# Folding the opening weights in another order, and splitting the late weights' preparation over two steps, in a two-layer fp32 pair kernel

## Chip, cores and metric

The kernel runs on one core of a Trainium2 chip. The metric is the device time of one execution in microseconds (us). Before the change four runs gave a median of 3333.75 us (3333.4 to 3334.44). Besides them there is one profiled execution, from which every duration below is taken.

The engines are named as the profile names them: PE is the matmul engine (TensorE) and PEld its weight loads, DVE is VectorE, ACT is ScalarE, POOL is GpSimd, SP is SyncE. A name with a "q" behind it (ACTq, SPq) is the engine's instruction queue, where DMA issues are shown.

## What is computed

`x` is a 384 x 384 field of 128 channels in fp32. Two layers follow each other:

```python
# layer 0
z = layernorm(x, norm_g, norm_b)
left  = (z @ Wl + bl) * sigmoid(z @ Wlg + blg)
right = (z @ Wr + br) * sigmoid(z @ Wrg + brg)
core  = einsum('bikh,bjkh->bijh', left, right)
zo    = layernorm(core, onorm_g, onorm_b) @ Wout + bout
x     = x + sigmoid(x @ Wg + bg) * zo
# layer 1
left  = x @ W_left + b_left + (x @ W_eq + b_eq)
right_sum = sum over the row of (x @ W_right + b_right)
out   = left * right_sum * sigmoid(x @ W_gate + b_gate)
out   = out @ W_out + b_out
y     = layernorm(out + x, ln_scale, ln_bias)
```

## The kernel before, in words

The work falls into three stages. Stage 1 (about 15 to 1146 us) makes `left` and `right` of layer 0; stage 2 (to 1889 us) is the einsum, channel by channel (L385 to L406); stage 3 is the rest, row by row (L610 to L663). The order of each engine's instructions is written out by hand: `seq` (L56) keeps program order on every engine.

Stage 1 reads `x` in 144 chunks of 8 tiles of 128 x 128 (`load_chunk`, L109) and works in 288 steps of 4 tiles, two steps to a chunk. For a step (n, q):

- `stats` (L215): mean and variance of the 4 tiles on DVE, in two halves.
- `powers` (L227): on POOL, the reciprocal root `rs` of the variance, by a power of -1/2, and `nd`, the mean less the root itself. It runs once for a chunk, at its second step, on 8 tiles.
- `shift` (L241): on POOL, z = x - nd, from two z buffers.
- `front` (L251): PE transposes z into a PSUM tile `pt` (two buffers), and ACT copies it to `zt`.
- `back` (L282), in two halves: PE multiplies `zt` with `wz`, the four weights side by side (L291), into a tile `pr` (three buffers); ACT takes the sigmoid of the gate half (L298); DVE multiplies both halves and the root into `lr` (L300).

The main loop (L328) runs, for step k: `shift` of step k+2, `powers` of k+5, `back` of k in two halves, with `front` of k+1 between them and `stats` of k+6 after each half. Then come SP's transfers: a chunk's load, the store of `zt`, a slice of `lr`. Ahead of the loop, six steps' statistics are taken (L316 to L327).

Two pieces of preparation lie around this:

- **The opening.** The layer norm's scale and shift are folded into the weights. ACT's queue issues the loads of the four weights, two columns (norm_g, norm_b), the four biases (one row each) and the chunks 2 to 5 (L129 to L135); only after that ACT loads its function table and warms it up (L144). `fold` (L148) on DVE brings weights and biases from the order l, r, lg, rg into pairs (l and r interleaved, then the gates), and PE adds up p1, the weights' column part with m1 = avg x (norm_b - norm_g), and the biases. `weights` (L164) makes wz = weights x norm_g + p1. All of the staging lies in one SBUF tile `stage`. `fold` comes after the second step's statistics, `weights` after the third's.
- **The late weights.** The weights of the later stages are loaded at step 4 (L346). After step 20, `late_weights` (L190) prepares them: on DVE m2 = -avg x onorm_g, on PE its product with Wout, on DVE wc from that, on PE Wout x onorm_b, on DVE bz; W_left += W_eq, and for each of three biases a product on PE and a subtraction on DVE. All five products go into one PSUM tile `pw`, which takes a `pt` buffer; m2 takes a z buffer.

Of the kernel before, what the change touches and what calls it, by code (L numbers as in the profile page):

```python
# [8 lines left out]
F32 = mybir.dt.float32  # L9
# [10 lines left out]
def triangle_then_gated_row_kernel(ctx: ExitStack, tc: tile.TileContext, a: dict, out: bass.AP):  # L20
# [35 lines left out]
    def seq(ins):  # L56

        return tc.keep_in_program_order(ins)
# [4 lines left out]
    def load(dst, src, queue=nc.sync):  # L63
        seq(queue.dma_start(out=dst, in_=src))
# [15 lines left out]
    with ExitStack() as ctx2:  # L80
# [15 lines left out]
        with tc.tile_pool(name="p1x", bufs=6, side="right") as xp, \  # L96
# [25 lines left out]


            stage = lrp.tile([P, H, G, 2], F32, tag="lr", name="stage").rearrange("p h i s -> p (h i s)")
            wst, wcat = stage[:, 0:4 * H], stage[:, 4 * H:8 * H]
            bst, bcat = stage[0:1, 8 * H:12 * H], stage[0:1, 12 * H:16 * H]
            m1, d = stage[:, 16 * H:17 * H], stage[:, 17 * H:17 * H + 1]
            sides = ("l", "r", "lg", "rg")
            for n, w in enumerate(sides):  # L129
                load(wst[:, n * H:(n + 1) * H], a["L0_conv_W" + w], nc.scalar)  # L130
            g0, b0 = column("L0_conv_norm_g", nc.scalar), column("L0_conv_norm_b", nc.scalar)
            for n, b in enumerate(sides):
                load(bst[:, n * H:(n + 1) * H], a["L0_conv_b" + b].rearrange("(o h) -> o h", o=1), nc.scalar)
            for n in range(2, 6):
                load_chunk(n, nc.scalar)  # L135
            ident = const([P, P], "ident")
# [6 lines left out]
            warm = const([P, 1], "warm")  # L143
            seq(nc.scalar.activation(warm, mhalf[:, 0:1], AF.Sigmoid))  # L144
            wz = const([P, 4 * H], "wz")
            p1 = pps.tile([P, 2, 4 * H], F32, tag="pr", name="p1")

            def fold():  # L148

                for t, st in ((wcat, wst), (bcat, bst)):  # L150
                    for g in range(2):
                        seq(nc.vector.tensor_copy(
                            t[:, g * 2 * H:(g + 1) * 2 * H].rearrange("p (h s) -> p s h", s=2),
                            st[:, g * 2 * H:(g + 1) * 2 * H].rearrange("p (s h) -> p s h", s=2),
                        ))

                seq(nc.vector.tensor_sub(d, b0, g0))
                seq(nc.vector.tensor_scalar(m1, avg, d, None, ALU.mult))  # L160
                seq(nc.tensor.matmul(p1[:, 0], lhsT=m1, rhs=wcat, start=True, stop=False))
                seq(nc.tensor.matmul(p1[:, 0], lhsT=avg[0:1, :], rhs=bcat, start=False, stop=True))

            def weights():  # L164
                seq(nc.vector.scalar_tensor_tensor(wz, wcat, g0, p1[:, 0], ALU.mult, ALU.add))

            wc = const([P, C], "wc")
            bz = const([P, 1], "bz")
# [21 lines left out]
            def late_weights():  # L190

                ps = tps.tile([P, 4, P], F32, tag="pt", name="pw")
                m2 = wp.tile([P, 4, C], F32, tag="z", name="m2", bufs=2)[:, 0]
                seq(nc.vector.tensor_scalar(m2, avg, go, -1.0, ALU.mult, ALU.mult))
                seq(nc.tensor.matmul(ps[:, 0], lhsT=m2, rhs=wout0, start=True, stop=True))
                seq(nc.vector.scalar_tensor_tensor(wc, wout0, go, ps[:, 0], ALU.mult, ALU.add))
                seq(nc.tensor.matmul(ps[:, 1, 0:1], lhsT=wout0, rhs=bo, start=True, stop=True))
                seq(nc.vector.tensor_add(bz, ps[:, 1, 0:1], bout0))  # L200

                seq(nc.vector.tensor_add(wleft, wleft, weq))
                seq(nc.vector.tensor_add(bleft, bleft, beq))
                for n, (w, b) in enumerate(((wleft, bleft), (wgate, bgate), (wright, bright))):
                    p4 = ps[:, 2, n:n + 1]
                    seq(nc.tensor.matmul(p4, lhsT=w, rhs=bout1, start=True, stop=True))
                    seq(nc.vector.tensor_sub(b, b, p4))
                seq(nc.vector.tensor_scalar(bright, bright, float(N), None, ALU.mult))  # L210

                seq(nc.vector.tensor_scalar(lns, lns, -1.0, None, ALU.mult))


            def stats(n, q, half):  # L215
# [11 lines left out]
            def powers(n, q):  # L227


                if q == NQ - 1:  # L230
                    _, mv, rs, sd = normed[n]
                    kb, ig, c = chunks[n]
                    if c == 0:
                        nds[kb, ig] = dp.tile([P, G], F32, tag="nd", name="nd")
                    nd = nds[kb, ig][:, c * XR:(c + 1) * XR]
                    seq(nc.gpsimd.tensor_scalar(sd, mv[:, :, 1], EPS, 1.0, ALU.add, ALU.mult))  # L236
                    seq(nc.gpsimd.tensor_tensor(rs, sd, mhalf[:, :XR], ALU.pow))
                    seq(nc.gpsimd.tensor_tensor(sd, sd, rs, ALU.mult))
                    seq(nc.gpsimd.tensor_tensor(nd, mv[:, :, 0], sd, ALU.subtract))

            def shift(n, q):  # L241

                kb, ig, c = chunks[n]
                z = wp.tile([P, 4, C], F32, tag="z", name="z", bufs=2)
                nd = nds[kb, ig][:, c * XR + 4 * q:c * XR + 4 * q + 4]
                seq(nc.gpsimd.tensor_tensor(  # L246
                    z, loaded[n][:, 4 * q:4 * q + 4, :], nd.unsqueeze(2).to_broadcast([P, 4, C]), ALU.subtract
                ))
                return z
# [66 lines left out]
            for k in range(AHEAD):  # L316
                for half in range(2):
                    stats(*steps[k], half)
                if k == 1:
                    fold()  # L320
                if k == 2:
                    weights()
                if k < AHEAD - 1:
                    powers(*steps[k])
                if k == 1:
                    zs = {j: shift(*steps[j]) for j in range(2)}
                    front(*steps[0], zs.pop(0))  # L327
            for k, (n, q) in enumerate(steps):  # L328
                if k + 2 < len(steps):
                    zs[k + 2] = shift(*steps[k + 2])  # L330
                if k + AHEAD - 1 < len(steps):
                    powers(*steps[k + AHEAD - 1])
                for half in range(2):
                    back(n, q, half)
                    if half == 0 and k + 1 < len(steps):
                        front(*steps[k + 1], zs.pop(k + 1))
                    if k + AHEAD < len(steps):
                        stats(*steps[k + AHEAD], half)
                if q == NQ - 1:
                    del loaded[n], normed[n]  # L340
                    load_chunk(n + 6)
                    if chunks[n][2] == G // XR - 1:
                        store_nd(*chunks[n][:2])
                store_zt(n, q)
                store_slice()
                if k == 4:  # L346
                    for t, src in later:
                        load(t, src)
                if k == 20:
                    late_weights()  # L350
                if k == len(steps) - 2 * G // 4 + 16:
                    assert not full
                    for h in range(2):
                        load_h(h)
# [338 lines left out]
```

## Time and profile before

| | us |
|---|---|
| median of four runs | 3333.75 (3333.4 to 3334.44) |
| profiled execution, its own time | 3332.9 |
| its span, first to last instruction | 3330.8 |
| PE busy | 3284.5 (99%) |
| DVE, POOL, ACT busy | 2499.2 (75%), 2234.8 (67%), 1949.5 (59%) |
| first matmul of L291 starts | 15.41 |
| late weights: first and last product start | 101.58, 105.49 |

The page of a profile gives busy times by engine, the chain of work that ended last, and the costliest groups of instructions; a row of a group ends in the idle time of the engine just before it and in what ended that idle time ("<-"). A row of the timeline is: start, duration, engine, line, operation, output<-inputs, shape, count ("x4" is four in a row), and in brackets the idle time before it. Matmuls in fp32 are recorded as two instructions each, and they overlap, so their spacing is read from the starts.

### The profile page before, as it was taken

The page shows a single profiled execution, that of the slowest core. Times are in us where ns is not written, and L with a number is a line of the kernel's source. Part 1 is how long each engine was busy: PE and PEld are TensorE (multiplying, and loading weights), DVE is VectorE, ACT ScalarE, POOL GpSimd, SP SyncE. Part 2 cuts the span into 40 slices and gives each one's busy share as a digit, 9 for nine tenths or more (in the row PEclk, how much of TensorE's full clock was granted, in tenths as well). Part 3 has the DMA queues.
Part 4 walks back from the last instruction along what each step waited for, and adds up shares of the span by engine and source line. Part 5 has one row for each costly group of instructions (what it writes and reads, how often), then busy time and mean ns, then how long its engine had stood idle before and what let it go on. Part 6 is the DMA issues. An engine that isn't in the chain of part 4 may idle for free.

```text
span 3330.8 us, 48534 instructions
## 1 busy us (share of the span) xinstructions
PE 3284.5 (99%) x12584; PEld 2005.5 (60%) x12584; DVE 2499.2 (75%) x8074; ACT 1949.5 (59%) x4049; POOL 2234.8 (67%) x3267
## 2 busy tenths in 40 slices
PE   8999999999999999999999999999999999999997
PEld 4444444444444566666666566777777777777775
DVE  6677777777777655554555578888888888888887
ACT  4455555555555433433433567777777777777776
POOL 5455555555555466555555378888888888888887
PEclk9999999999999999999999999999999999999999
DMA  5899899899999498999999888889888988998883
GB/s 150 241 282 283 251 282 278 257 282 272 263 281 266 146 284 284 281 282 285 281 284 285 273 266 249 270 274 276 265 272 274 272 269 272 276 269 269 274 269 95
DMA packets 924619, 872.93 MB, mean 262 GB/s; under 512 B 24868, under 2 KB 839720, under 8 KB 924344
## 3 DMA queue, kind: packets, MB, share of 16 engines
q1 hardware_dynamic: 904960, 794.32, 76.3%
q0 software_dynamic: 13152, 71.37, 10.5%
q10 hardware_dynamic: 6232, 4.13, 0.4%
q8 instruction: 103, 1.69, 0.2%
q14 instruction: 172, 1.41, 0.1%
HBM read 507.85 MB, written 361.89 MB: 261 GB/s over the span
## 4 chain that ended last, share of the span: by engine, by line
PE 62%; ACT 1%; POOL 1%; DVE 0%; issue 0%; DMA 0%; POOLq 0%; SPq 0%; ACTq 0%
PE pc L392 22%; PE pr L530 7%; PE py L559 7%; PE pg L493 7%; PE pl L548 7%; PE pg L547 7%; PE py L560 4%; ACT py L590 1%; POOL rs L579 0%; PE pq L514 0%; DMA xt<-nd_d 0%; POOL yt L602 0%; PE pxt L506 0%; DVE yt L601 0%; DVE st L574 0%
## 5 line engine op out<-in xcount | busy, mean ns | idle before, releaser
L291 PE MATMUL pr<-wz,zt 128*128 128x512 f32 x2304 | 1042.7, 594 | 0.7 <-ACT zt L257 0.7
L298 ACT ACTIVATE sg<-pr,rs 128x256 f32<-128x256 f32 x1152 | 482.7, 470 | 508.1 <-PE pr L291 375.4
L392 PE MATMUL pc<-rr,lrh 128*128 128x384 f32 x2304 | 743.3, 486 | 1.9 <-DVE lr L300 1.9
L300 DVE SCALAR_TENSOR_TENSOR lr<-pr,rs,sg 128x256 f32<-128x256 f32 x1152 | 504.7, 480 | 275.0 <-ACT sg L298 227.1
L291 PEld LDWEIGHTS pr<-wz,zt 128*128 128x128 f32 x2304 | 415.2, 191 | 412.4 <-issue 346.8
L392 PEld LDWEIGHTS pc<-rr,lrh 128*128 128x128 f32 x2304 | 452.0, 196 | 293.2 <-issue 2.5
L590 ACT ACTIVATE py<-py,nm,rs 128x128 f32<-128x128 f32 x1152 | 494.4, 429 | 184.0 <-POOL rs L583 90.4
L401 DVE TENSOR_TENSOR csum<-csum,ct 128x1152 f32<-128x1152 f32 x128 | 178.9, 1398 | 347.1 <-ACT ct L398 347.1
L559 PEld LDWEIGHTS py<-wo,u 128*128 128x128 f32 x2304 | 377.5, 191 | 102.4 <-ACT wo L541 1.7
L398 ACT COPY ct<-pc 128x1152 f32<-128x1152 f32 x128 | 143.2, 1119 | 450.4 <-PE pc L392 446.7
L602 POOL TENSOR_TENSOR yt<-yt,lnb 128x384 f32<-128x384 f32 x384 | 404.8, 1054 | 2.9 <-DVE yt L601 2.6
L521 POOL TENSOR_TENSOR cs<-ct,rt 128x384 f32<-128x384 f32 x384 | 405.0, 1059 | 0.9 <-PE pr L530 0.9
L559 PE MATMUL py<-wo,u 128*128 128x128 f32 x2304 | 403.0, 275 | 1.2 <-ACT wo L541 1.2
L378 POOL COPY rr<-lrh 128x768 f32<-128x768 f32 x128 | 176.2, 1376 | 309.0 <-DMA lrh<-lr_d 299.8
L574 DVE BATCH_NORM_STATS2 st<-py 128x6 f32<-128x128 f32 x1152 | 265.9, 286 | 96.5 <-PE py L560 95.9
L246 POOL TENSOR_TENSOR z<-xt,nd 128x512 f32<-128x512 f32 x288 | 299.8, 1041 | 43.4 <-POOL z L246 30.7
L530 PE MATMUL pr<-cs,wc 128*128 128x384 f32 x768 | 318.8, 497 | 2.9 <-POOL cs L521 2.9
L236 POOL TENSOR_SCALAR sd<-mv 128x8 f32<-128x8 f32 x144 | 28.3, 197 | 436.9 <-DVE mv L225 436.9
L560 PE MATMUL py<-ident,x1T 128*128 128x128 f32 x1152 | 314.0, 273 | 0.0
L548 PE MATMUL pl<-x1T,mat_L_conv_W_left 128*128 128x384 f32 x768 | 311.5, 487 | 1.2 <-ACT gT L495 1.2
L547 PE MATMUL pg<-x1T,mat_L_conv_W_gate 128*128 128x384 f32 x768 | 311.5, 487 | 0.9 <-DVE x1T L533 0.5
L493 PE MATMUL pg<-xt,mat_L_conv_Wg 128*128 128x384 f32 x720 | 292.0, 487 | 0.0
(96 smaller groups left out, 4912.2 us busy)
## 6 DMA issues: line engine op xcount, KB each, us to landing
lr_d<-lr SPq DMA_DIRECT2D x128, 1024.0 KB, 7.2
lrh<-lr_d SPq DMA_DIRECT2D x128, 768.0 KB, 7.8
xt_d<-zt SPq DMA_DIRECT2D x288, 256.0 KB, 5.3
ct<-core_d SPq DMA_DIRECT2D x96, 768.0 KB, 6.6
rt<-rstd_d SPq DMA_DIRECT2D x96, 768.0 KB, 8.1
out_dram<-yt SPq DMA_DIRECT2D x95, 768.0 KB, 4.9
core_d<-ct SPq DMA_DIRECT2D x125, 576.0 KB, 8.8
xt<-in_x_dram SPq DMA_DIRECT2D x140, 512.0 KB, 6.9
```

Of the source, the lines that this page charges most:

```text
L291: seq(nc.tensor.matmul(pr[:, r, :], lhsT=zts[n, q][:, 2 * half + r, :], rhs=wz, start=True, stop=True))
L298: seq(nc.scalar.activation(sg[r], pr[:, r, 2 * H:], AF.Sigmoid, scale=rs[r]))
L300: seq(nc.vector.scalar_tensor_tensor(t[:, :, c * XR + r0 + r, :], pr[:, r, :2 * H].rearrange("k (h s) -> k h s", s=2), rs[r], sg[r].rearra ...
L392: seq(nc.tensor.matmul(pc[:, ib, :N], lhsT=t[:, kb, ib * P:(ib + 1) * P, 0], rhs=rr[:, kb], start=(kb == 0), stop=(kb == NB - 1),))
L493: seq(nc.tensor.matmul(pg[:, :N], lhsT=wg0, rhs=r["xT"], start=True, stop=True))
L521: seq(nc.gpsimd.tensor_tensor(cs, ct[:, i % RG], rt[:, i % RG], ALU.mult))
L530: seq(nc.tensor.matmul(pr[:, :N], lhsT=wc, rhs=r["cs"], start=True, stop=True))
L547: seq(nc.tensor.matmul(pg2[:, :N], lhsT=wgate, rhs=r["x1T"], start=True, stop=True))
L548: seq(nc.tensor.matmul(pl[:, :N], lhsT=wleft, rhs=r["x1T"], start=True, stop=True))
L559: seq(nc.tensor.matmul(py[:, s], lhsT=r["u"][:, s], rhs=r["wo"], start=True, stop=False))
L560: seq(nc.tensor.matmul(py[:, s], lhsT=r["x1T"][:, s], rhs=ident, start=False, stop=True, is_transpose=True))
L590: seq(nc.scalar.activation(py[:, s], py[:, s], AF.Identity, bias=nm[:, n, b:b + 1], scale=rs[:, n, b:b + 1]))
```

## The change

In the opening, the biases are loaded to all 128 partitions, so that each bias load writes 64 KB instead of one row. The weights are no longer re-ordered before the fold: DVE scales the biases by 1/C and computes wst = wst x norm_g + bst in the order loaded, PE makes a single product p1 from m1 and wst, and the pairing happens when `weights` adds the two (two additions). The first chunk's roots are taken for each step by itself, on 4 tiles. `fold` comes after the first step's statistics, `weights` after the second's, and shift and front of step 0 come before the second step's statistics.

The late weights are split. After step 20, DVE makes m2, adds W_eq and b_eq and negates ln_scale. After step 21, PE makes all five products, and DVE then reads them all.

```diff
-            wst, wcat = stage[:, 0:4 * H], stage[:, 4 * H:8 * H]
-            bst, bcat = stage[0:1, 8 * H:12 * H], stage[0:1, 12 * H:16 * H]
-            m1, d = stage[:, 16 * H:17 * H], stage[:, 17 * H:17 * H + 1]
+            wst, bst = stage[:, 0:4 * H], stage[:, 4 * H:8 * H]
+            m1, d = stage[:, 8 * H:9 * H], stage[:, 9 * H:9 * H + 1]
...
-                load(bst[:, n * H:(n + 1) * H], a["L0_conv_b" + b].rearrange("(o h) -> o h", o=1), nc.scalar)
+                load(bst[:, n * H:(n + 1) * H], a["L0_conv_b" + b].partition_broadcast(P), nc.scalar)
...
-            p1 = pps.tile([P, 2, 4 * H], F32, tag="pr", name="p1")
+            p1 = pps.tile([P, 2, 4 * H], F32, tag="pr", name="p1")[:, 0]
 
             def fold():
-
-                for t, st in ((wcat, wst), (bcat, bst)):
-                    for g in range(2):
-                        seq(nc.vector.tensor_copy(
-                            t[:, g * 2 * H:(g + 1) * 2 * H].rearrange("p (h s) -> p s h", s=2),
-                            st[:, g * 2 * H:(g + 1) * 2 * H].rearrange("p (s h) -> p s h", s=2),
-                        ))
                 seq(nc.vector.tensor_sub(d, b0, g0))
                 seq(nc.vector.tensor_scalar(m1, avg, d, None, ALU.mult))
-                seq(nc.tensor.matmul(p1[:, 0], lhsT=m1, rhs=wcat, start=True, stop=False))
-                seq(nc.tensor.matmul(p1[:, 0], lhsT=avg[0:1, :], rhs=bcat, start=False, stop=True))
+                seq(nc.tensor.matmul(p1, lhsT=m1, rhs=wst, start=True, stop=True))
+                seq(nc.vector.tensor_scalar(bst, bst, 1.0 / C, None, ALU.mult))
+                seq(nc.vector.scalar_tensor_tensor(wst, wst, g0, bst, ALU.mult, ALU.add))
 
             def weights():
-                seq(nc.vector.scalar_tensor_tensor(wz, wcat, g0, p1[:, 0], ALU.mult, ALU.add))
+
+                for g in range(2):
+                    gs = slice(g * 2 * H, (g + 1) * 2 * H)
+                    seq(nc.vector.tensor_add(
+                        wz[:, gs].rearrange("p (h s) -> p s h", s=2),
+                        wst[:, gs].rearrange("p (s h) -> p s h", s=2),
+                        p1[:, gs].rearrange("p (s h) -> p s h", s=2),
+                    ))
...
-                ps = tps.tile([P, 4, P], F32, tag="pt", name="pw")
                 m2 = wp.tile([P, 4, C], F32, tag="z", name="m2", bufs=2)[:, 0]
                 seq(nc.vector.tensor_scalar(m2, avg, go, -1.0, ALU.mult, ALU.mult))
-                seq(nc.tensor.matmul(ps[:, 0], lhsT=m2, rhs=wout0, start=True, stop=True))
-                seq(nc.vector.scalar_tensor_tensor(wc, wout0, go, ps[:, 0], ALU.mult, ALU.add))
-                seq(nc.tensor.matmul(ps[:, 1, 0:1], lhsT=wout0, rhs=bo, start=True, stop=True))
-                seq(nc.vector.tensor_add(bz, ps[:, 1, 0:1], bout0))
                 seq(nc.vector.tensor_add(wleft, wleft, weq))
                 seq(nc.vector.tensor_add(bleft, bleft, beq))
-                for n, (w, b) in enumerate(((wleft, bleft), (wgate, bgate), (wright, bright))):
-                    p4 = ps[:, 2, n:n + 1]
-                    seq(nc.tensor.matmul(p4, lhsT=w, rhs=bout1, start=True, stop=True))
-                    seq(nc.vector.tensor_sub(b, b, p4))
+                seq(nc.vector.tensor_scalar(lns, lns, -1.0, None, ALU.mult))
+                return m2
+
+            def late_products(m2):
+                ps = tps.tile([P, 4, P], F32, tag="pt", name="pw")
+                own = ((wleft, bleft), (wgate, bgate), (wright, bright))
+                seq(nc.tensor.matmul(ps[:, 0], lhsT=m2, rhs=wout0, start=True, stop=True))
+                seq(nc.tensor.matmul(ps[:, 1, 0:1], lhsT=wout0, rhs=bo, start=True, stop=True))
+                for n, (w, b) in enumerate(own):
+                    seq(nc.tensor.matmul(ps[:, 2, n:n + 1], lhsT=w, rhs=bout1, start=True, stop=True))
+                seq(nc.vector.scalar_tensor_tensor(wc, wout0, go, ps[:, 0], ALU.mult, ALU.add))
+                seq(nc.vector.tensor_add(bz, ps[:, 1, 0:1], bout0))
+                for n, (w, b) in enumerate(own):
+                    seq(nc.vector.tensor_sub(b, b, ps[:, 2, n:n + 1]))
                 seq(nc.vector.tensor_scalar(bright, bright, float(N), None, ALU.mult))
-                seq(nc.vector.tensor_scalar(lns, lns, -1.0, None, ALU.mult))
...
-                if q == NQ - 1:
+                if n == 0 or q == NQ - 1:
+                    lo, hi = (4 * q if n == 0 else 0), 4 * q + 4
                     _, mv, rs, sd = normed[n]
+                    mv, rs, sd = mv[:, lo:hi], rs[:, lo:hi], sd[:, lo:hi]
...
-                if k == 1:
-                    fold()
-                if k == 2:
-                    weights()
                 if k < AHEAD - 1:
                     powers(*steps[k])
+                if k == 0:
+                    fold()
+                    zs[0] = shift(*steps[0])
+                    front(*steps[0], zs.pop(0))
                 if k == 1:
-                    zs = {j: shift(*steps[j]) for j in range(2)}
-                    front(*steps[0], zs.pop(0))
+                    weights()
+                    zs[1] = shift(*steps[1])
...
                 if k == 20:
-                    late_weights()
+                    m2 = late_weights()
+                if k == 21:
+                    late_products(m2)
```

More of the change, by code (lines that the diff above doesn't have):

```diff
@@ L227, in powers @@
             def powers(n, q):
-                if q == NQ - 1:
+                if n == 0 or q == NQ - 1:
+                    lo, hi = (4 * q if n == 0 else 0), 4 * q + 4
                     _, mv, rs, sd = normed[n]
+                    mv, rs, sd = mv[:, lo:hi], rs[:, lo:hi], sd[:, lo:hi]
                     kb, ig, c = chunks[n]
-                    if c == 0:
+                    if c == 0 and lo == 0:
                         nds[kb, ig] = dp.tile([P, G], F32, tag="nd", name="nd")
-                    nd = nds[kb, ig][:, c * XR:(c + 1) * XR]
+                    nd = nds[kb, ig][:, c * XR + lo:c * XR + hi]
                     seq(nc.gpsimd.tensor_scalar(sd, mv[:, :, 1], EPS, 1.0, ALU.add, ALU.mult))
-                    seq(nc.gpsimd.tensor_tensor(rs, sd, mhalf[:, :XR], ALU.pow))
+                    seq(nc.gpsimd.tensor_tensor(rs, sd, mhalf[:, :hi - lo], ALU.pow))
                     seq(nc.gpsimd.tensor_tensor(sd, sd, rs, ALU.mult))
```

## The prediction

> **What bounds the kernel now.** I read the page first: TensorE (PE) is busy 99% of the span, and the chain that ended last is PE for 62% of it. Its costliest group, the four-weight product of stage 1, has waited 0.7 us in 2304 matmuls:
>
> ```profile
> L291 PE MATMUL pr<-wz,zt 128*128 128x512 f32 x2304 | 1042.7, 594 | 0.7 <-ACT zt L257 0.7
> ```
>
> So stage 1 is one unbroken row of matmuls once it runs, and a change to it can pay only where PE stands still or runs slowly. The waits of PE before 150 us name the places (columns: us in total, times, longest):
>
> ```profile
> PE p L161 <- DVE stage L160: 9.6, 1, 9.6
> PE pw L197 <- issue: 2.7, 1, 2.7
> PE pr L291 <- ACT zt L257: 0.7, 1, 0.7
> PE pw L208 <- DVE mat_L_conv_W_left L204: 0.5, 1, 0.5
> PE pw L199 <- DVE wc L198: 0.4, 1, 0.4
> ```
>
> Both are what the diff touches: the opening, and the late weights after step 20. The windows view prices the second (us, busy us of PE, PEld, DVE, ACT, POOL, granted clock, DMA share, GB/s): clock 0.50 for 10.24 us.
>
> ```profile
> 101.01:111.25 10.24, 8.28 (x20) 5.07 (x21) 2.64 (x15) 1.43 (x3) 1.60 (x2) 0.50 1.08 308
> 111.25:115.00 3.75, 3.75 (x13) 1.90 (x12) 2.25 (x11) 1.35 (x4) 0.48 (x1) 1.00 1.00 283
> ```
>
> The timeline of PE shows the order there:
>
> ```profile
> 97.04 1.88 PE L291 MATMUL pr<-wz,zt 128*128 128x512 f32 x4
> 101.58 0.76 PE L197 MATMUL pw<-mat_L_conv_Wout,m 128*128 128x128 f32 x2 [2.67 <-issue]
> 102.79 0.59 PE L199 MATMUL pw<-col_L_conv_onorm_b,mat_L_conv_Wout 128*128 128x1 f32 x2 [0.44 <-DVE wc L198]
> ...
> 105.94 3.76 PE L291 MATMUL pr<-wz,zt 128*128 128x512 f32 x4
> ...
> 114.67 3.60 PE L291 MATMUL pr<-wz,zt 128*128 128x512 f32 x8
> ```
>
> A step takes 3.875 us (its groups of eight start at 93.17, 97.04 and later 114.67, 118.55). Undisturbed, the group at 114.67 would have started at 97.04 + 2 x 3.875 = 104.79. **The late weights cost 9.88 us**: PE stands 2.67 us until VectorE (DVE) has made m2, the five products alternate with DVE until 105.94 (4.36 us), and the rest, 2.85 us, is matmuls at half clock until 111.25.
>
> The opening in the timeline of all engines:
>
> ```profile
> 7.85 4.09 ACTq L114 DMA_DIRECT2D xt<-in_x_dram  x4
> 11.97 1.28 ACT L144 ACT_TABLE_LOAD   x1 [11.97 <-DMA xt<-in_x_dram]
> 13.26 0.20 ACT L144 ACTIVATE warm<-mhalf 128x1 f32<-128x1 f32 x1
> 13.73 0.75 DVE L165 SCALAR_TENSOR_TENSOR wz<-stage,col_L_conv_norm_g,p 128x512 f32<-128x512 f32 x1 [2.97 <-PE p L162]
> 14.77 0.58 ACT L257 COPY zt<-pt 128x512 f32<-128x512 f32 x1 [1.31 <-PE pt L255]
> 15.41 3.78 PE L291 MATMUL pr<-wz,zt 128*128 128x512 f32 x4 [0.68 <-ACT zt L257]
> ```
>
> The stream starts at 15.41, released by the first zt copy; but ScalarE (ACT) was itself free only at 13.46, behind four tile loads that it issues and its table load. There is 1.31 us to win before ACT becomes the bound.
>
> **Part 1, late weights a step ahead.** At step 20 only DVE works now: m2 0.25, wleft 0.28, bleft 0.15, lns 0.22, together 0.9 us beginning at 101.23, where m2 stands today. PE goes straight on into step 21, whose second half would end at 97.04 + 3.875 + 4 x 0.43 = 102.63. By then m2 (101.48) and wleft (about 101.75) are ready with 0.9 us to spare, so the products wait for nothing. They follow each other without a DVE read between: today's waits of 0.44, 0.45, 0.25 and 0.25 us for DVE reads of the same PSUM tile go. Price on a warm PE: a pair of 128x128 (L559) advances the stream by 0.22 us. The 128x4 pair of stage 3 (L514) together with its successor takes 2607.95 to 2608.82 = 0.87 us against 0.65 for that successor alone, so 0.22. Five products are 5 x 0.22 = 1.1 us. Bounds: 0.8 if the small ones cost only the 0.14 us from the start of L514 to the next matmul, 2.2 if the weight loads don't overlap (0.43 each). I take 1.1, the nearest row. DVE's reads behind them (wc 0.35, bz 0.16, three 0.16, 0.15: 1.1 us) lie in step 21 to 22.
>
> Who is queued behind this: DVE is busy 739.6 of 968 us in the quiet stretch, 2.96 us of each step, so 0.9 us just fits step 20 and 1.1 fits the lengthened step 21; the copies into lr that stand behind them release pr buffers only three halves later, some 1.8 us after they are due. m2 now holds one of the two z buffers for a step, so on POOL shift(23) waits for front(22) or for the product: z is then ready by about 104.2, and front(23) needs it at about 105.4. pw takes a pt buffer that is read out by then and gives it back before front(24). All this costs nothing while these 1 to 2 us last; if one is used up, PE waits its excess. Gain: 9.88 - 1.1 = **8.8 us** (7.7 to 9.1).
>
> [...] Here PE had stopped at 98.92 and the clock fell at 101.01, after 2.1 us. [...] The row shows 0.50, so 8.8 stands; it also says that a pause of 2 us left at step 21 would cost the half clock again.
>
> **Part 2, opening.** (a) The four re-ordering copies on DVE (0.33, 0.33, 0.28, 0.28) and the bias product (2.07 us on PE, 11.62 to 13.69) go. (b) The first roots are taken on four tiles: DVE finishes them at about 6.5 instead of 7.65, and the power on 8 columns takes 1.64, on 6 (stage 3) 1.33, so on 4 about 1.0 (estimate). z of step 0 is done near 9.6 instead of 11.45. (c) m1 needs norm_b, which lands at about 8.0: m1 at 8.5, product 2.08 us, transposes 1.1 us, so pt is ready at 11.8 instead of 14.7. (d) DVE: bst scaling 128x512, estimated 0.4 from 0.22 to 0.29 for 128 columns and 0.33 for a copy of 256 (0.3 to 0.75); then 0.75 for the fold, which must follow both the last bias and the product's read of wst (10.65). The last bias is issued near 7.75; a 64 KB matrix lands 1.9 us and the broadcast lns 3.4 us after issue, so 9.7 to 11.2, the fold at 11.4 to 12.4; stats of step 1 take 1.2, two additions from PSUM 0.48 each: wz at 13.5 to 14.5. (e) ACT: each bias is now 128 rows, 64 KB instead of 0.5. The issues of the last two grow from 0.25 towards the weights' 0.45 to 0.61, 0.4 to 0.7 us ahead of the tile loads; 256 KB at 290 GB/s are 0.9 us, of which most fits the time in which the DMA engines stand idle (7.2 to 8.7 us). ACT is late by 0.4 to 1.6; I take 0.6. Then zt is ready at 13.46 + 0.6 + 0.64 = 14.7, later than wz.
>
> So the stream starts near 14.7 instead of 15.41: 0.7 earlier, not the three that pt gains. Matmuls are 0.86 to 0.95 us apart, half speed, until 19.1; if that instant stays, half of 0.7 counts, if it moves along, all. I take **0.5 us** (-0.5 with ACT at its late end, +0.9). Step 2's z, moved behind the fold, is ready by 20.5 at worst and needed at 22.9. The extra four small POOL operations lie beside DMA waits.
>
> **Sum.** 8.8 + 0.5 = 9.3 us, all on PE ahead of a stretch in which PE never waits (968 of 968 us busy from 160 to 1128). Span 3330.8 to 3321.5, own time 3332.9 to 3323.6. The median stands 0.85 above that execution: 3333.75 - 9.3 = **3324.5 us**.
>
> **Rivals.**
> 1. *Gain as summed*, 0.81: 3322 to 3327. With it, 0.06: the opening loses 1 us, and 3326.
> 2. *A wait takes the old one's place at step 21*: a product or front(23) waits over 2 us and the clock halves again. Then only the alternation is saved: 9.88 - (2.67 + 2.2 + 2.85) = 2.2, plus 0.5: 3331. For: the z buffer is tight. Against: every operand has 0.9 us. 0.05.
> 3. *The transfers take the gain back*: DMA is at a share of 0.93 from 160 to 1128, and the gain could return as a wait for the next stage's loads: 3333. Against: no wait of PE in that stretch, and its rate moves between 206 and 318 GB/s. 0.03.
> 4. *Slower*: without the 10 us pause, lr stores and x loads collide in steps 16 to 32, and an x tile comes after its statistics are due. Tiles are loaded five steps (19.4 us) ahead and land 4.1 to 9.8 us after issue, so it decides from another 9.6 us of lateness. Each such stall costs at least 2.1 us of wait and 2.7 of half clock; four make 19 us, 3324.5 + 19 = 3344. 0.05.
>
> **Numbers.** 0.2% is 6.7 us, about what a measurement of this kernel can tell from no change, so faster means under 3327.1: 0.87. Within: 0.08. Slower: 0.05. The range takes the bounds (7.2 to 10.0 us of gain: 3323.7 to 3326.6) and, on each side, some 1.5 us for the spread of the four runs (1.0) and for where the clock's changes fall at the two later changes of stage: 3322.0 to 3328.0.
>
> **What would show it.** After: no wait at the products, five pairs in 1.1 us, clock 1.00 throughout 95 to 115, step groups 3.875 us apart but for one of about 5.0; the first L291 at 14.5 to 15.0, released by ACT, with ACT's issues ending at 12.3 to 12.7. Wrong if the clock row shows 0.50 after step 21, if the first L291 is released by DVE wz after 15.4, or if PE waits for POOL z in steps 21 to 24.

## The result and the profile after

| | before | after |
|---|---|---|
| median, us (runs) | 3333.64 (51) | 3327.01 (33) |
| lowest to highest | 3330.25 to 3335.30 | 3325.13 to 3328.35 |
| profiled execution: own time, span | 3332.9, 3330.8 | 3328.28, 3326.1 |
| first stage-1 matmul starts | 15.41 | 16.45 |
| step 20's second half starts | 97.04 | 99.22 |
| step 22's second half starts | 114.67 | 108.09 |
| first matmul of stage 2 to the end | 2184.63 | 2186.51 |

The ratio is 0.9981 [0.9976, 0.9986]: 6.6 us faster, where 9.3 were forecast. The table also takes the profiled pair apart. The opening does not win 0.5 us, it loses: the stream is 2.18 us later at step 20. The late weights win 8.78 us between step 20 and step 22. From step 22 to stage 2's first matmul both kernels take 1031.48 us. Behind it, 1.88 us are lost again. That leaves 4.7 us for this pair, not 6.6: the profiled execution of the kernel after, 3328.28 us, is the second slowest of its 33. So the sizes of the parts are taken below from several profiles.

In the new file the stage-1 product is L297 (L291 before), its zt copy L263, the fold's product L153, the bias scaling L154, the fold L155, wz L161, the table load L143, m2 L195, the late products L208 to L211 and DVE's reads of them L212 to L216.

The page's row of the stage-1 product shows the new loss, 4.8 us of waiting where it was 0.7:

```profile
L297 PE MATMUL pr<-wz,zt 128*128 128x512 f32 x2304 | 1041.3, 594 | 4.8 <-ACT zt L263 4.8
```

The waits of PE in the kernel after no longer have a row of a `pw` product, of which there were five (2.7, 0.5, 0.4 and twice 0.2 us). What is left ahead of stage 2 is the opening:

```profile
PE p L153 <- DVE stage L152: 8.8, 1, 8.8
PE pr L297 <- ACT zt L263: 4.8, 1, 4.8
```

**Late weights.** The timeline of PE in the kernel after, at step 21:

```profile
103.10 1.88 PE L297 MATMUL pr<-wz,zt 128*128 128x512 f32 x4
104.82 0.38 PE L208 MATMUL pw<-mat_L_conv_Wout,m 128*128 128x128 f32 x2
105.04 0.28 PE L209 MATMUL pw<-col_L_conv_onorm_b,mat_L_conv_Wout 128*128 128x1 f32 x2
...
105.85 1.96 PE L297 MATMUL pr<-wz,zt 128*128 128x512 f32 x4
108.09 3.60 PE L297 MATMUL pr<-wz,zt 128*128 128x512 f32 x8
```

No row has a bracket, so nothing waited. The first product starts 1.72 us after the half step and the stream goes on at 105.85: five pairs in 1.03 us. Undisturbed, the last group would start at 99.22 + 2 x 3.875 = 106.97; it starts at 108.09. I call this excess the late cost below: 1.1 us, where it was 9.9. The clock held; windows view of the kernel after (us, busy us of PE, PEld, DVE, ACT, POOL, granted clock, DMA share, GB/s), here and in the opening:

```profile
105.00:108.50 3.50, 3.50 (x19) 2.28 (x19) 3.29 (x18) 1.44 (x4) 1.72 (x3) 1.00 1.10 330
12.21:15.62 3.41, 0.00 (x0) 0.00 (x0) 2.73 (x12) 1.19 (x1) 0.19 (x1) 1.00 1.13 291
16.40:22.45 6.05, 6.00 (x10) 2.93 (x11) 5.40 (x34) 1.37 (x3) 5.25 (x11) 0.50 0.81 223
```

The last two rows say that the clock had been full from 12.21 on and fell at 15.62, while PE waited, so that the stream starts at half clock, 0.50 until 22.45; before, full clock came at 19.09. This explains the 2.18 us at step 20: the start is 1.04 us later, and the time at half clock behind it is 6.00 us instead of 3.68, of which half counts, 1.16.

**Opening.** The timeline of all engines in the kernel after:

```profile
8.11 6.29 ACTq L114 DMA_DIRECT2D xt<-in_x_dram  x4
...
12.79 0.43 DVE L154 TENSOR_SCALAR stage<-stage 128x512 f32<-128x512 f32 x1 [4.09 <-DMA stage<-in_L_conv_brg_dram]
13.31 0.75 DVE L155 SCALAR_TENSOR_TENSOR stage<-stage,col_L_conv_norm_g 128x512 f32<-128x512 f32 x1
...
14.43 1.28 ACT L143 ACT_TABLE_LOAD   x1 [14.43 <-DMA xt<-in_x_dram]
...
15.18 0.72 DVE L161 TENSOR_TENSOR wz<-stage,p 128x256 f32<-128x256 f32 x2
...
15.83 0.57 ACT L263 COPY zt<-pt 128x512 f32<-128x512 f32 x1
...
16.45 3.78 PE L297 MATMUL pr<-wz,zt 128*128 128x512 f32 x4 [4.76 <-ACT zt L263]
```

Two chains are late, and the biases' loads are at the root of both. DVE stands 4.09 us until the last bias has landed: it was issued at 7.62 and its last piece came at 12.67, 5.05 us later (the list of DMA issues rounds: KB, us from issue to landing).

```profile
stage<-in_L_conv_brg_dram ACTq DMA_DIRECT2D x1, 64.0 KB, 5.0
```

And ACT's four tile-load issues take 6.29 us instead of 4.09, so the table load starts at 14.43 instead of 11.97 and the zt copy at 15.83 instead of 14.77. Either chain alone would have lost: zt is ready at 16.40 and wz at 15.90, both behind the 15.41 of before. The transposes have been ready since 11.69 (four from 10.63, 1.06 us): what the fold in another order wins is there, and waits.

### The profile page after: what moved, and what is told of

It reads as the page before. It is cut to its first block, busy times and chain, and to the rows that moved or that the text cites. A ratio compares the mean times of both kernels' runs of the same rounds, so it can differ in the third digit from the quotient of the medians.

```text
span 3326.1 us, 48532 instructions
## 1 busy us (share of the span) xinstructions
PE 3280.5 (99%) x12582; PEld 2004.4 (60%) x12582; DVE 2499.4 (75%) x8073; ACT 1949.5 (59%) x4049; POOL 2237.8 (67%) x3271
## 2 busy tenths in 40 slices
DMA packets 925188, 873.19 MB, mean 263 GB/s; under 512 B 24929, under 2 KB 840289, under 8 KB 924913
## 4 chain that ended last, share of the span: by engine, by line
PE 63%; ACT 1%; POOL 1%; DVE 0%; issue 0%; DMA 0%; POOLq 0%; SPq 0%; ACTq 0%
PE pc L400 22%; PE pr L538 7%; PE py L567 7%; PE pg L501 7%; PE pl L556 7%; PE pg L555 7%; PE py L568 4%; ACT py L598 1%; POOL rs L587 0%; PE pq L522 0%; DMA xt<-nd_d 0%; POOL yt L610 0%; PE pxt L514 0%; DVE yt L609 0%; DVE st L582 0%
## 5 line engine op out<-in xcount | busy, mean ns | idle before, releaser
L297 PE MATMUL pr<-wz,zt 128*128 128x512 f32 x2304 | 1041.3, 594 | 4.8 <-ACT zt L263 4.8
L297 PEld LDWEIGHTS pr<-wz,zt 128*128 128x128 f32 x2304 | 414.8, 191 | 416.2 <-issue 346.7
L242 POOL TENSOR_SCALAR sd<-mv 128x8 f32<-128x8 f32 (+1 forms) x145 | 28.5, 197 | 436.1 <-DVE mv L229 435.9
```

What stands on the lines that cost most here:

```text
L297: seq(nc.tensor.matmul(pr[:, r, :], lhsT=zts[n, q][:, 2 * half + r, :], rhs=wz, start=True, stop=True))
```

## The experiments

All are measured against the kernel before on the same chip. "Stream" is the start of the first stage-1 matmul in the experiment's profile.

| kernel | median us (runs) | ratio to before | stream | late cost | stage 2 to end |
|---|---|---|---|---|---|
| after | 3327.01 (33) | 0.9981 [0.9976, 0.9986] | 16.45 | 1.11 | 2186.51 |
| late_only | 3326.42 (14) | 0.9979 [0.9972, 0.9987] | 15.53 | 1.11 | 2186.82 |
| opening_only | 3335.06 (13) | 1.0004 [0.9996, 1.0012] | 16.54 | 8.49 | 2184.75 |
| row_bias | 3326.35 (10) | 0.9977 [0.9968, 0.9986] | 14.55 | 1.11 | 2186.47 |
| bias_rows_apart | 3325.70 (10) | 0.9976 [0.9967, 0.9986] | 14.57 | 1.11 | 2186.21 |
| together_at_20 | 3332.90 (12) | 0.9994 [0.9986, 1.0003] | 16.40 | 7.05 | 2186.38 |
| alternating_at_21 | 3333.18 (12) | 0.9999 [0.9990, 1.0007] | 16.39 | 7.03 | 2186.47 |
| row_bias_tiles_sp | 3330.82 (13) | 0.9990 [0.9982, 0.9998] | 19.31 | 1.11 | 2186.69 |
| row_bias_tiles_sp_heat | 3331.21 (13) | 0.9993 [0.9985, 1.0001] | 19.26 | 1.11 | 2186.99 |
| row_bias_heat | 3325.12 (10) | 0.9974 [0.9964, 0.9983] | 16.03 | 1.11 | 2188.41 |
| before, three more profiles | 3333.92, 3333.88, 3332.86 (1 each) | | 15.39, 16.10, 15.35 | 8.50, 9.91, 9.36 | 2186.34, 2184.92, 2185.59 |

### Each part alone

late_only is the kernel before with the late weights of the change:

```diff
 if k == 20:
-    late_weights()
+    m2 = late_weights()
+if k == 21:
+    late_products(m2)
```

> The opening of the kernel before, with the late weights split over two steps. My theory: the split alone gives the 8.8 us that its rows add up to, and the new opening takes some 2.2 us of it back: 3333.6 - 8.8 = 3324.8 us, first stage-1 matmul at 15.4, five products in 1.1 us, clock 1.00 throughout. Rival (the opening is neutral and the split gives only the 6.6 us that the whole change gave): 3327.0 us.

opening_only is the change with the late weights of before:

```diff
 if k == 20:
-    m2 = late_weights()
-if k == 21:
-    late_products(m2)
+    late_weights()
```

> The new opening with the late weights as before. My theory: first stage-1 matmul at 16.4 instead of 15.4, one window more at half clock, 2.2 us in all: 3333.6 + 2.2 = 3335.8 us. Rival (opening neutral): 3333.6 us.

The late weights alone give 3326.42, 7.5 us of gain. The opening alone gives 3335.06, 1.1 us slower by the medians; its interval includes no change, but the profile shows the same delay as the change does, stream at 16.54 and step 20 at 98.98. So the gain is all the late weights', and the opening starts the stream later instead of earlier. The size of that loss is less than the 2.18 us of the profiled pair, and near the noise: four profiles with the new opening have step 20's second half at 97.89, 97.99, 98.98 and 99.22 (mean 98.52), five with the old one (the four of before and late_only) have it at 96.59, 97.04, 97.77, 97.89 and 98.16 (mean 97.49), 1.0 apart.

The spread has two parts. In 13 of the 14 profiles, step 20's second half starts 79.77 to 79.80 us after the start of the stream plus half of the time that the stream ran at half clock (row_bias_heat, below, has 0.4 more). The start differs by 0.9 us between the two openings (mean 16.44 and 15.56); the time at half clock varies from 2.9 to 6.0 us among these nine, with no clear difference (mean 4.6 and 4.3).

### What in the bias loads is slow

Three causes were open: the source read 128 times, the 256 KB as such, and the new order of the opening. row_bias loads the biases as single rows again and adds them on PE, as before the change, but keeps everything else of the new opening:

```diff
-load(bst[:, n * H:(n + 1) * H], a["L0_conv_b" + b].partition_broadcast(P), nc.scalar)
+load(bst[0:1, n * H:(n + 1) * H], a["L0_conv_b" + b].rearrange("(o h) -> o h", o=1), nc.scalar)
...
-matmul(p1, lhsT=m1, rhs=wst, start=True, stop=True)
-tensor_scalar(bst, bst, 1.0 / C, None, ALU.mult)
-scalar_tensor_tensor(wst, wst, g0, bst, ALU.mult, ALU.add)
+matmul(p1, lhsT=m1, rhs=wst, start=True, stop=False)
+matmul(p1, lhsT=avg[0:1, :], rhs=bst[0:1, :], start=False, stop=True)
...
-tensor_add(wz_pairs, wst_pairs, p1_pairs)
+scalar_tensor_tensor(wz_pairs, wst_pairs, g0, p1_pairs, ALU.mult, ALU.add)
```

> The changed kernel, but each bias is again loaded as one row and added by a second product on PE; weights still in the order loaded, roots by four tiles, late weights split. Theory A (the biases' broadcast loads hold up the tile loads behind them on ACT's queue, and DVE's fold) and theory B (the same by their bytes and rows, whatever they read): ACT is free at 13.5, the first stage-1 matmul starts at 14.1 to 14.3, time 3324.8 less 0.6 to 1.2, so 3323.6 to 3324.2 us. Theory C (the new order on DVE and PE is what delays): the first matmul stays at 16 or later, 3327 us.

bias_rows_apart keeps the change as it is, with its 64 KB for each bias on the same queue, but reads 128 different rows (those of the weights) instead of one row 128 times. It leaves the biases themselves out, so its results are wrong and only its time is of use:

```diff
-load(bst[:, n * H:(n + 1) * H], a["L0_conv_b" + b].partition_broadcast(P), nc.scalar)
+load(bst[:, n * H:(n + 1) * H], a["L0_conv_W" + b], nc.scalar)
```

> The changed kernel with the four bias loads reading 128 different rows each (the weights' rows stand in for the biases, so the bias term is replaced by other numbers): the same bytes, rows and queue, but no row read 128 times. Theory A (a row read 128 times arrives slowly): the last of the four lands by 9.7 to 10.3 instead of 12.7, ACT's issues end near 12.5 instead of 14.4, first stage-1 matmul at 14.7, 3324.5 us. Theory B (bytes and rows): landing 12.7, first matmul 16.4, 3327.0 us.

With the single rows the stream starts at 14.55, so it is not the new order that is late. The timeline of row_bias; ACT's issues take 4.10 us again:

```profile
7.89 4.10 ACTq L114 DMA_DIRECT2D xt<-in_x_dram  x4
...
14.55 3.78 PE L296 MATMUL pr<-wz,zt 128*128 128x512 f32 x4 [0.67 <-DVE st L226]
```

And the timeline of bias_rows_apart, with as many bytes in as many rows as the change:

```profile
8.10 4.10 ACTq L114 DMA_DIRECT2D xt<-in_x_dram  x4
...
9.65 0.43 DVE L154 TENSOR_SCALAR stage<-stage 128x512 f32<-128x512 f32 x1
...
11.83 0.75 DVE L155 SCALAR_TENSOR_TENSOR stage<-stage,col_L_conv_norm_g 128x512 f32<-128x512 f32 x1 [1.76 <-PE p L153]
12.23 1.28 ACT L143 ACT_TABLE_LOAD   x1 [12.23 <-DMA xt<-in_x_dram]
...
14.57 3.75 PE L297 MATMUL pr<-wz,zt 128*128 128x512 f32 x4 [1.92 <-DVE wz L161]
```

From its list of DMA issues:

```profile
stage<-in_L_conv_Wrg_dram ACTq DMA_DIRECT2D x1, 64.0 KB, 1.9
```

L154 has lost its bracket of 4.09 us. The last of the four loads landed at 9.52, 1.9 us after its issue at 7.62, against 5.05 us in the change; the first tile load behind it landed at 12.37 instead of 14.56, and ACT was free 2.2 us sooner (table load at 12.23). Bytes, rows, queue and order are equal in the two kernels (both profiles count 925188 DMA packets), only the source differs. So one row read 128 times is what costs 3.1 us on DVE's chain and 2.2 on ACT's. The first two of the four loads land alike (8.31 and 8.48 against 8.37 and 8.58); the last two come at 10.45 and 12.67 instead of 9.15 and 9.52. Why the DMA engines are slow at it no run here shows.

Both medians, 3326.35 and 3325.70, lie below the change's 3327.01, but the three intervals overlap: 1.9 us of stream start are not 1.9 us of time, since the clock rose at 20.66 and 18.99 in these two, and step 20 was reached at 97.38 and 96.55, 1.1 and 2.0 us ahead of the mean of the new opening.

### Why both halves of the late change are needed

together_at_20 has the products in a row, but in step 20, right behind m2; alternating_at_21 has m2 a step ahead, but a DVE read between each product and the next, as before:

```diff
 if k == 20:
-    m2 = late_weights()
-if k == 21:
-    late_products(m2)
+    late_products(late_weights())
```

> The changed kernel, but the five products run in a row right after step 20, where PE has to wait for m2. It tells how much of the late gain is the alternation and how much the wait with its half clock. My theory (the wait of 2.67 us stays and halves the clock for two or three windows, so 1.4 to 2.8 us besides; the products in a row cost 1.1 to 2.2): the late part costs 5.5 to 7.5 us instead of 1.1, time 3327.0 + 4.4 to 6.4 = 3331.4 to 3333.4 us. Rival (the alternation was the cost, the wait alone leaves the clock full): 2.7 + 1.1 = 3.8, 3329.7 us and clock 1.00 there.

```diff
 matmul(ps[:, 0], lhsT=m2, rhs=wout0)
-matmul(ps[:, 1, 0:1], lhsT=wout0, rhs=bo)
-for n, (w, b) in enumerate(own):
-    matmul(ps[:, 2, n:n + 1], lhsT=w, rhs=bout1)
 scalar_tensor_tensor(wc, wout0, go, ps[:, 0], ALU.mult, ALU.add)
+matmul(ps[:, 1, 0:1], lhsT=wout0, rhs=bo)
 tensor_add(bz, ps[:, 1, 0:1], bout0)
 for n, (w, b) in enumerate(own):
+    matmul(ps[:, 2, n:n + 1], lhsT=w, rhs=bout1)
     tensor_sub(b, b, ps[:, 2, n:n + 1])
```

> The changed kernel, with m2 a step ahead, but after step 21 each product is again followed by DVE's read before the next product. My theory (each of the five round trips leaves PE idle 0.3 to 0.5 us, too little to halve the clock): the late part costs 3.5 to 4.2 us instead of 1.1, time 3329.5 to 3330.0 us, clock 1.00 there. Rival (the short waits alone halve the clock): 1.4 to 2.8 more, 3331 to 3333 us.

Each half alone saves 2.4 of the 9.4 us: late cost 7.05 and 7.03 us. Their medians, 3332.90 and 3333.18, are 2.2 and 1.9 below opening_only, which has the same opening, and not shown to differ from the kernel before. For together_at_20 that was expected. For alternating_at_21 I had expected 3329.5 to 3330 and missed. The timeline of PE in together_at_20:

```profile
97.99 1.88 PE L297 MATMUL pr<-wz,zt 128*128 128x512 f32 x4
102.54 0.77 PE L208 MATMUL pw<-mat_L_conv_Wout,m 128*128 128x128 f32 x2 [2.67 <-issue]
...
104.67 3.76 PE L297 MATMUL pr<-wz,zt 128*128 128x512 f32 x4
```

and in alternating_at_21:

```profile
101.77 1.88 PE L296 MATMUL pr<-wz,zt 128*128 128x512 f32 x4
103.48 0.38 PE L208 MATMUL pw<-mat_L_conv_Wout,m 128*128 128x128 f32 x2
106.60 0.38 PE L210 MATMUL pw<-col_L_conv_onorm_b,mat_L_conv_Wout 128*128 128x1 f32 x2 [2.73 <-DVE wc L209]
107.24 0.38 PE L213 MATMUL pw<-col_L_conv_b_out,mat_L_conv_W_left 128*128 128x1 f32 x2 [0.25 <-DVE bz L211]
```

The pause of some 2.7 us is the same, one product further on. The first product now finds m2 ready, but the second waits for wc, and wc (DVE L209, 106.23 to 106.55) stands on DVE's queue behind two halves' copies into lr and their statistics (103.46 to 106.3), just as m2 had stood behind those of step 20. In the kernel before wc followed m2 directly on that queue, so its wait was short (0.44). Taking away one wait uncovers the other; only the change, which has neither, saves 8.3 us.

### How constant the cost of before is

The kernel before, unchanged, three more times, for its profile:

> The kernel before, profiled once more. The late part cost 9.89 us in its first profile (three windows at half clock) and 8.49 in the kernel with only the new opening (two). If three windows are the rule, 9.9 again; if it depends on where the clock's grid falls, 8.4 to 9.9.

> As the run before it: the late part costs 9.9 us if three windows are the rule, 8.4 to 9.9 if it depends on where the clock's grid falls.

> As the two runs before it: the late part costs 9.9 us if three windows are the rule, 8.4 to 9.9 if it depends on where the clock's grid falls.

The windows view around the late weights, in the first, second and third of them:

```profile
102.77:109.59 6.82, 5.43 (x14) 3.33 (x13) 1.53 (x9) 0.00 (x0) 1.04 (x1) 0.50 1.08 319
```

```profile
101.78:112.02 10.24, 8.31 (x20) 5.10 (x21) 2.63 (x15) 1.43 (x3) 1.63 (x2) 0.50 1.07 310
```

```profile
103.58:110.41 6.83, 6.58 (x14) 3.81 (x15) 1.49 (x7) 1.43 (x3) 0.82 (x1) 0.50 1.13 341
```

The same 2.67 us pause costs two or three pieces of 3.41 us at half clock, in whole pieces. The late cost of the four profiles is 9.89, 8.50, 9.91 and 9.36 us, mean 9.4; my forecast took the 9.88 of a single one. The stretches at half clock are 10.24 us long in before and before_again_b (three pieces) and 6.82 and 6.83 us in before_again_a and before_again_c (two), so the number varies from run to run of one program.

The traces show more of it. In each of the 14 profiles all changes of the granted clock lie a whole number of such pieces apart (19.09 and 101.01 in the first of before: 24; 15.62 and 1886.13 in after: 548). Cut along this grid, before_again_c reads:

```profile
96.76:100.17 3.41, 1.71 (x4) 0.41 (x3) 2.51 (x11) 1.80 (x5) 2.24 (x4) 1.00 1.13 341
100.17:103.58 3.41, 1.25 (x7) 0.92 (x7) 1.85 (x11) 0.00 (x0) 1.04 (x1) 1.00 0.98 244
103.58:106.99 3.41, 3.16 (x7) 2.04 (x8) 0.60 (x4) 0.00 (x0) 0.00 (x0) 0.50 1.15 347
106.99:110.41 3.42, 3.42 (x8) 1.76 (x8) 0.90 (x3) 1.43 (x3) 0.82 (x1) 0.50 1.11 335
```

After a piece with PE idle for 1.7 us the clock held. After one with 2.2 us idle it fell, though PE had been at work again since 101.14. It rose only behind a piece that was busy throughout (3.42). In all seven profiles in which the clock fell at the late weights, PE had been idle 2.05 to 2.67 us of the piece before (2.09 in before, 2.67 in before_again_a, 2.16 in before_again_c); elsewhere in the traces falls begin at 1.72 us idle (1.84 and 1.90 in before, in the pieces from 1913.49 and 1889.60), and pieces without a fall go up to 1.85. So in these profiles some 1.7 to 1.9 us of idle time, about half a piece, was enough, and where the pause lies on the grid sets its price.

### Trying for a better opening

In row_bias ACT is free at 13.50 and the zt copy starts at 13.91, behind the fold's two products (4.1 us, against 2.1 in row_bias_heat) and the transposes. row_bias_tiles_sp moves the chunks' issues from ACT to SP; row_bias_tiles_sp_heat adds five filler products on PE ahead of the fold, to have the clock up early; row_bias_heat is row_bias with six fillers at the start and three after step 0's front. Their result is read by nobody.

```diff
-    load_chunk(n, nc.scalar)
+    load_chunk(n)
```

> Biases as rows, and the chunks 2 to 5 issued by SP instead of ACT. Theory A says that ACT's issues were the bound of the opening only with the broadcasts; with rows ACT (13.5) and PE's two products with the transposes (pt at 13.9) are level. So without the tile loads ACT waits for pt: first stage-1 matmul at 14.4 to 14.6, as with rows alone (14.55), 3326.0 us. Rival (ACT is still the bound): first matmul at 13.7, 3325.2 us.

```diff
+hot = stage[:, 12 * H:16 * H]
+memset(hot, 0.5)
+for _ in range(5):
+    matmul(p01[:, 1], lhsT=avg, rhs=hot, start=True, stop=True)
```

> The same, and PE makes five products of a constant tile from about 1.7 us on, whose result nothing reads, so that it is busy until the fold. My theory (the half clock of the opening costs 2 to 3 us: in the fold's two products and the transposes, 5.2 us at half speed, and in the stream until 19 to 22): the fold's products take 2.1 instead of 4.1 us, the first stage-1 matmul starts at 12.0 to 12.6 at full clock, 3 to 4 us less than with rows alone: 3322.0 to 3323.2 us. Rival (step 2's z on POOL, not ready before 17.8, takes back what PE gains): 3324.5 us, with a wait of PE for z in step 1.

```diff
+heat(6)
...
 front(*steps[0], zs.pop(0))
+heat(3)
```

> Rows for the biases with the tile loads left on ACT's queue (as in the run with rows alone, 3326.35 us, first stage-1 matmul 14.55, half clock until 20.7), and PE made busy by products of a constant tile that nothing reads: six from 1.6 us to the fold, three between the transposes and the stream. My theory (half clock is what the opening still pays): the fold's two products take 2.1 instead of 4.1 us, the first stage-1 matmul waits for ACT and starts at 14.0 to 14.3, at full clock from its start; half of 14.55 to 20.7 is 3.1 us, so 3.1 to 3.6 us less: 3322.7 to 3323.3 us. Rival (step 2's z on POOL, at 19.8 there, is needed at 18.6 then and PE waits for it): 1.2 us less of it, 3324.2 us.

The first two are 4.5 and 4.9 us slower than row_bias, and no theory of mine had that. The timeline of row_bias_tiles_sp:

```profile
0.73 8.67 SPq L114 DMA_DIRECT2D xt<-in_x_dram  x6
...
6.71 0.33 ACTq L64 DMA_DIRECT2D col_L_conv_norm_b<-in_L_conv_norm_b_dram  x1
...
11.84 0.16 DVE L151 TENSOR_TENSOR stage<-col_L_conv_norm_b,col_L_conv_norm_g 128x1 f32<-128x1 f32 x1 [5.24 <-DMA col_L_conv_norm_b<-in_L_conv_norm_b_dram]
...
15.55 1.19 PE L154 MATMUL p<-stage,avg 1*128 1x512 f32 x1 [1.11 <-DMA stage<-in_L_conv_brg_dram]
```

With SP free to issue all six chunks, their loads go ahead of ACT's small ones: norm_b is issued at 6.71 instead of 3.58, DVE waits 5.24 us for it, and the last bias arrives at 15.5. The traces also show what holds the issue back: the loads of the opening share eight completion semaphores, and one behind the first eight is issued only when the one that used its semaphore has landed (in after, bl is issued at 4.30, when the first weight has landed at 4.28, and br and blg at 5.21 and 7.25, behind landings at 5.19 and 7.23). norm_b, no longer among the first eight, waits for that of the second weight, which landed at 6.69. In row_bias, before and after, ACT's own order had kept four of the six chunks behind the small loads. The heated version has the same bound (the fold's first product at 12.41), and its fillers ended at 7.78; the clock had fallen again at 11.71, before the fold: it says nothing about a full clock in the opening.

The timeline of row_bias_heat:

```profile
12.23 2.74 PE L152 MATMUL p<-stage,avg 128*128 128x512 f32 x6
...
15.01 0.87 DVE L169 SCALAR_TENSOR_TENSOR wz<-stage,col_L_conv_norm_g,p 128x256 f32<-128x256 f32 x2 [5.27 <-PE p L152]
...
16.03 1.95 PE L305 MATMUL pr<-wz,zt 128*128 128x512 f32 x4 [1.06 <-DVE wz L169]
```

The stream starts at full clock (four matmuls in 1.95 us instead of 3.78), but at 16.03 instead of row_bias's 14.55: wz waits until the three fillers are done (14.97), though they write the other half of p1's PSUM tile. zt was ready at 14.06, so without that wait the stream could have started in the 14.0 to 14.3 that I expected (not tried). Net, step 20's second half starts at 96.20, 1.2 us ahead of row_bias, and the median of 3325.12, the lowest of all, is 1.2 us below row_bias too; I had expected some 2 us less. The profiled execution itself took 3327.19, the slowest of ten: stages 2 and 3 took 2188.41 us, 1.9 more than in row_bias, and it alone of the 14 profiles has a piece at half clock at the start of stage 2 (1137.24 to 1140.66). The interval of its ratio overlaps those of row_bias, bias_rows_apart and late_only, so none of these four is shown to beat the others; all four have lower medians than the change.

## Why the prediction was right and where it failed

The time, 3327.01, lies in the range of 3322 to 3328, 2.5 us above the forecast, and rival 1 came, with the opening's loss. That it lies there is owed to the late weights and to the width of the range: the opening's gain was forecast with the wrong sign, and a loss of 1.1 us behind stage 1 was not in the sum.

**Part 1, late weights: right in mechanism and in price.** Five pairs took 1.03 us (1.1 from the groups' own spacing), priced at 1.1, no wait, clock 1.00, groups 3.875 apart but for one of 4.99. What was mis-sized is the term subtracted from: 9.88 is one execution's number, and the mean over four profiles of before is 9.4, so the gain is 8.3 and not 8.8. late_only measured a gain of 7.5, and the difference of late costs is 7.4 to 8.8 us in every pair of profiles, so the row, with its half clock in the price, was a fair guide; but how many pieces at half clock that row held was chance.

**Part 1, margins: thinner than forecast.** The forecast gave every operand 0.9 us. The timelines of DVE and POOL in the kernel after:

```profile
103.42 1.05 DVE L195 TENSOR_SCALAR m<-avg,col_L_conv_onorm_g 128x128 f32<-128x128 f32 x1
```

```profile
103.34 1.04 POOL L252 TENSOR_TENSOR z<-xt,nd 128x512 f32<-128x512 f32 x1 [1.15 <-PE pt L261]
```

m2, 0.25 us before, took 1.05 and was done at 104.47, just behind POOL's z (104.38). Of the 0.9 us only 0.35 were left when its product started at 104.82. DVE's four operations together took 1.45 us and not 0.9. In all eight kernels with m2 a step ahead of its product, m2 runs beside POOL's z and takes 1.04 to 1.05 us (1.05 in after and alternating_at_21, 1.04 in late_only). The like operation m1 of the opening shows it from both sides: 0.29 us in the change (8.42 to 8.71), where z starts only at 8.54, and 1.16 (8.51 to 9.67) in bias_rows_apart, where z runs from 8.54 to 9.58. So the delay comes beside z; in bias_rows_apart it fell on m1, though that is recorded 0.03 us ahead of z, and z kept its 1.04 us. The m1 of the kernel before took 0.29 us in the middle of POOL's root (8.10 to 9.77). Why z delays it no run here shows. The prediction left it out; it would have taken 0.8 us from the margin. It cost nothing here because 0.35 us remained.

**Part 2, opening: parts (a) to (c) right, (d) and (e) wrong.** POOL's power on four columns took 1.04 us (1.0 estimated), z of step 0 ended at 9.60 (9.6), pt was ready at 11.69 (11.8). The step that failed is the landing of the biases: "9.7 to 11.2", with 1.9 to 3.4 us from issue, taken from a 64 KB matrix and from lns. Measured: 12.67, 5.05 us. From it follow the fold at 13.31 (11.4 to 12.4 forecast), wz ready at 15.9 (13.5 to 14.5), and ACT late by 2.46 us (0.4 to 1.6). bias_rows_apart, with distinct rows, gives the 1.9 us that I had taken, ends ACT's issues at 12.20 and starts the stream at 14.57, against 14.7 forecast: the sum held for the load that I had priced, not for the load that is there. It held with some luck, as wz came last there, 0.2 us behind zt, and the forecast had zt last. I had lns, itself a broadcast, as the upper end at 3.4, but it was a single one; four in a row behind each other on one row were not in the trace of before.

**The rest.** Rivals 3 and 4 are refuted: 1031.48 us from step 22 to stage 2 in every profile, so neither the transfers nor new stalls take anything back. Rival 2's wait did not come in the change; alternating_at_21 shows it one edit away, 2.73 us for wc, at 3333.18 where I gave 3331.

**The sum as measured.** Late weights -8.3, opening +1.0, stages 2 and 3 +1.1: -6.2, against -6.6 measured. The last term is the mean of late_only, row_bias, bias_rows_apart and the change (2186.5) less that of four profiles of before (2185.4). In the profiled pair it lies at the start of stage 3 (stage 2 takes 743.28 us in both), where PE waits briefly and one stretch of half clock lasted 6.83 us after and 3.41 before. The windows view of after, then of before:

```profile
1896.37:1903.19 6.82, 6.09 (x16) 3.95 (x17) 6.61 (x9) 4.21 (x9) 1.13 (x2) 0.50 0.63 202
```

```profile
1903.25:1906.66 3.41, 2.98 (x7) 1.94 (x8) 3.34 (x4) 2.29 (x6) 0.81 (x1) 0.50 0.76 251
```

Before ranges from 2184.6 to 2186.3, the four others from 2186.2 to 2186.8; opening_only, with the late weights of before, has 2184.75, but together_at_20 and alternating_at_21, whose late cost is still high, have 2186.4 and 2186.5. Whether the term belongs to the late weights' earlier end or to chance in where the clock's grid falls stays open.

## What to carry to other kernels

When a small preparation must pass between two engines in mid-stream, count every crossing: a product that needs DVE and a DVE result that the next product needs are two waits in series on one queue, and moving only one of them ahead uncovers the other (2.4 us saved of 9.4, instead of 8.3). Price a load by a row with the same source pattern, not the same bytes: a broadcast row (one row read for all partitions) is another load than a matrix (5.05 us from issue to landing against 1.9 for the last of four here). Take the price of a pause from several profiles, as the half clock behind it came in whole pieces of 3.41 us here, two or three behind the same pause in the four profiles of before. And when loads are moved to another queue, look first at which small loads the old order had let through.

## What the runs showed of the hardware

- Of four loads that each read one 512-byte row into 128 partitions, the last landed 5.05 us after issue (after); with 128 different rows it took 1.9 us (bias_rows_apart). The first tile load behind them landed 2.2 us later in after (14.56 against 12.37).
- A pause of 2.7 us on PE cost one piece of 3.41 us at half clock (alternating_at_21) to three (before, before_again_b), 7.0 to 9.9 us in all with the waits and products behind it, depending on the run and on what followed it.
- In the 14 profiles the granted clock changed only on a grid of 3.41 us, and fell at the late weights after pieces in which PE was idle 2.05 to 2.67 us. It held there after pieces with 1.3 us (alternating_at_21) and 1.7 us (before_again_c) idle.
- A 128x128 operation on DVE (tensor_scalar) took 1.04 to 1.05 us (m2, eight kernels) and 1.16 us (m1 in bias_rows_apart) beside POOL's z instead of 0.25 (m2 in before) and 0.29 (m1 in before and after).
- DVE's read of one half of a PSUM tile waited for matmuls in its other half (wz in row_bias_heat, 0.04 us after they ended at 14.97). Whether the chip needs that or only the kernel's bookkeeping of the tile, no run here shows.
